# Sixteen DRAM copies of the B and C rows, and last states that enter a scan through its first token

## Chip, cores and metric

The kernel runs on one core of a Trainium2 chip. The metric is the device time of one execution in microseconds (us); the time before is the median of three runs, 13002.54 us (12999.16 to 13004.72). The engines are named as in the profile: PE is TensorE with its weight loads (PEld), DVE is VectorE, ACT is ScalarE, POOL is GpSimd, and SP is SyncE, which issues the DMA transfers. DMA transfers run on 16 DMA engines.

## What is computed

The input is two images of 96 channels and 128 x 128 pixels. A layer normalization over the channels is followed by a mixer, two feed-forward blocks in rounded arithmetic and a 3 x 3 convolution between them. Nearly all of the time goes to the mixer, which sends the 16384 pixels of an image, as a sequence, through four state-space scans: by rows, by rows backwards, by columns, by columns backwards. Cut to what matters, one scan is:

```
def _mamba(x, in_w, conv_w, conv_b, xproj_w, dt_w, dt_b, A_log, Dp, outp_w):
    xc, z = jnp.split(x @ in_w.T, 2, axis=-1)           # 192 channels each
    xc = silu(causal_conv4(xc) + conv_b)
    xdbl = xc @ xproj_w.T
    dt_raw, Bm, Cm = xdbl[..., :6], xdbl[..., 6:22], xdbl[..., 22:]
    dt = softplus(dt_raw @ dt_w.T + dt_b)
    A = -jnp.exp(A_log)                                 # 192 channels x 16 states
    def step(h, t):
        dt_t, u_t, B_t, C_t = t
        h = exp(dt_t[:, :, None] * A) * h + dt_t[:, :, None] * B_t[:, None, :] * u_t[:, :, None]
        return h, einsum('bds,bs->bd', h, C_t)
    _, ys = jax.lax.scan(step, h0, (dt, xc, Bm, Cm))
    y = (ys + Dp * xc) * silu(z)
    return y @ outp_w.T
```

For every token and every one of 16 states, B and C are one number each, the same for all 192 channels of a direction.

## The kernel before

For each of two images, `normalize` writes the normalized image to DRAM by rows and by columns, `mamba` does the four scans, and `ffn_and_conv` the rest. `mamba` takes the directions in two pairs (the two forward ones, then the two backward ones). A pair's 2 x 192 channels lie in three groups of 128 partitions: group 0 is of the first direction, group 2 of the second, and group 1 has 64 channels of each. The sequence is cut into 32 pieces of 512 tokens. A step is one piece of one pair, so there are 64 steps for an image and 128 in all.

A step has 24 units: for each group, eight pairs of states. For one unit:

- POOL multiplies dt * u by the two rows of B (`b_part`, line 324, 128 x 1024).
- ACT makes the two decays exp(dt * A) (`decay`, line 330) in PSUM.
- DVE runs two scans of 512 tokens (`scan`, line 334), in place in the decays' tile. The state at the end of the preceding piece is the scan's initial value, read per partition from the tile `hst`; in the first step of a pair it is the constant 0.0.
- DVE multiplies both results by the rows of C (line 409), ACT saves the last states in `hst` (line 410), and PE sums the products over the states into y by products with the identity (`sums`, line 341).

When a group ends, DVE multiplies y by the gate (`gated`, line 349), and after groups 1 and 2 PE projects the result (`project`) and ACT adds it to the image in `collect`.

The rows of B and C must stand in all 128 partitions. `rows_out` (line 255) copies 64 rows of 512 tokens, 32 for B and 32 for C, from PE's result into SBUF (partitions 32 to 95 of the tile `rows`) and writes them to DRAM (`bcd`), in four copies by four transfers (line 261). `row_tile` (line 312) then reads tiles of 128 partitions x 4 rows x 512 tokens (1 MiB, 8 KB a partition) with one transfer for groups 0 and 2, in which partition p reads copy p mod 4, and two transfers of 64 partitions for group 1. One tile serves two units; there are 12 for B and 12 for C in a step. A tile of B is asked for 6 units ahead, one of C 4 units ahead, each into a ring of tiles, so that a transfer waits until an old tile has been used.

All engines run in the order in which the program issues: the schedule is written out by hand in the loop over k, the units of all steps (lines 436 to 457). In turn k the loop issues, in this order: a fetch of B (for unit k + 6, at even k), POOL's multiply of unit k + 2 (`feed`), the work put down for (k, 0), the first scan of unit k, the multiply by C and the rest of unit k - 1 (`behind`), the second scan of unit k, a fetch of C (for unit k + 4), the decays of unit k + 2 (`feed_decay`), and the work put down for (k, 1). The work put down is the prologue of the next step (lines 301 to 310): convolution and gate on PE, in turns 4 to 7, 10 and 11; silu on ACT in turns 8 and 14; the rows in turn 12; and for each group the softplus that makes dt, begun in turns 13, 18 and 21, whose last four instructions (`dt_q`, `dt_log`, `dt_sum`, `dt_u`; lines 287 to 297, 128 x 512) run on POOL between its multiplies.

Of the kernel before, what the change touches and what calls it, by code (L numbers as in the profile page):

```python
# [10 lines left out]
F32 = mybir.dt.float32  # L11
# [3 lines left out]
AF = mybir.ActivationFunctionType  # L15
ALU = mybir.AluOpType
# [7 lines left out]
T = 512  # L24
NT = L // T
R = T // W
S = 16
# [2 lines left out]
HID = 384  # L30
PAIRS = ((0, 2), (1, 3))
NG = 3
COPIES = 4
B_AHEAD = 3
C_AHEAD = 2
AHEAD = 2
# [1 line left out]
BCO = 32  # L38
NBC = 4 * S
# [3 lines left out]
def tile_metaformer(ctx: ExitStack, tc: tile.TileContext, a: dict, out: bass.AP):  # L43
    nc = tc.nc
# [30 lines left out]
    amat = cpool.tile([128, 2, NG, S], F32, name="amat")  # L75
# [107 lines left out]
    def mamba(acc, xnr, xnc):  # L183

        with ExitStack() as st:
            pool = lambda n, bufs, **kw: st.enter_context(tc.tile_pool(name=n, bufs=bufs, **kw))
            io, one, two, gen = pool("io", 1), pool("one", 1), pool("two", 2), pool("gen", 4)
            ps_w, ps_y, ps_m = (pool(n, k, space=PSUM) for n, k in (("ps_w", 3), ("ps_y", 1), ("ps_m", 1)))
            rows_d = pool("rows_d", 3, space=DRAM)

            hst = one.tile([128, NG, S], F32, name="hst")
            acc_w = acc.rearrange("c (h w) -> c w h", w=W)

            def misc():
# [15 lines left out]
            def prologue(pi, i, d):  # L210
# [3 lines left out]
                src = []  # L214
# [40 lines left out]
                def rows_out():  # L255

                    d["rows"] = one.tile([BCO + NBC, T], F32, name="rows")
                    nc.scalar.copy(d["rows"], d["ps"][0 : BCO + NBC, :])
                    d["bcd"] = rows_d.tile([COPIES, 2, NBC // 2, T], F32, name="bcd")
                    for n in range(COPIES):  # L260
                        nc.sync.dma_start(d["bcd"][n].rearrange("k r t -> (k r) t"), d["rows"][BCO:, :])

# [35 lines left out]

                at = [(0, 0, load), (8, 1, partial(silu, "xc")), (14, 1, partial(silu, "sz"))]
                at += [(12, 0, rows), (12, 1, rows_out)]
                for g, k in enumerate((4, 5, 6)):
                    at += [(k, 0, partial(conv, g)), (k, 1, partial(conv_out, g))]
# [7 lines left out]
            def row_tile(d, g, s, k, ahead):  # L312

                t = gen.tile([128, 4, T], F32, name=f"row{k}", bufs=ahead + 1)
                for half in range(2) if g == 1 else (slice(None),):
                    rows = slice(half * 64, half * 64 + 64) if g == 1 else half
                    at = s + S * (half if g == 1 else g // 2)
                    n = (64 if g == 1 else 128) // COPIES
                    src = d["bcd"][None, :, k, at : at + 4, :].broadcast_to((n, COPIES, 4, T))
                    nc.sync.dma_start(t[rows], src)  # L320
                return t

            def b_part(d, g, b):
                nc.gpsimd.tensor_tensor(b, d["dtu"][g][:, None, :].broadcast_to((128, 2, T)), b, ALU.mult)  # L324

            def decay(pi, d, g, s):

                da = ps_w.tile([128, 2, T], F32, name="da")
                for j in range(2):
                    nc.scalar.activation(da[:, j, :], d["dt"][g], AF.Exp, scale=amat[:, pi, g, s + j : s + j + 1])  # L330
                return da

            def scan(i, g, s, j, da, b, h):
                nc.vector.tensor_tensor_scan(  # L334
                    h[:, j, :], da[:, j, :], b[:, j, :],
                    0.0 if i == 0 else hst[:, g, s + j : s + j + 1], ALU.mult, ALU.add,
                )

            def sums(s, y, c):
                for j in range(2):  # L340
# [27 lines left out]
            steps = [(pi, i) for pi in range(2) for i in range(NT)]  # L368
            units = [(g, s) for g in range(NG) for s in range(0, S, 2)]
            nu = len(units)  # L370
            total = nu * len(steps)
            state = [{} for _ in steps]
            todo = {}

            def later(k, where, f, *args):
                todo.setdefault((k, where), []).append(partial(f, *args))

            def issue(k, where):
                for f in todo.pop((k, where), ()):
                    f()  # L380
# [3 lines left out]
            bs, cs, das, hs = {}, {}, {}, {}  # L384

            def fetch(k, n, ahead, m):
                if k < total:
                    t = row_tile(state[k // nu], *units[k % nu], n, ahead)
                    m[k], m[k + 1] = t[:, 0:2, :], t[:, 2:4, :]

            def feed(k):
                if k < total:
                    n = k // nu
                    b_part(state[n], units[k % nu][0], bs[k])

            def feed_decay(k):
                if k < total:
                    n = k // nu
                    das[k] = decay(steps[n][0], state[n], *units[k % nu])
# [3 lines left out]
            def behind(k):  # L403

                n, u = divmod(k, nu)
                (pi, i), d, (g, s) = steps[n], state[n], units[u]
                h, c = hs.pop(k), cs.pop(k)
                if (g, s) not in BY_POOL:
                    nc.vector.tensor_tensor(c, h, c, ALU.mult)  # L409
                nc.scalar.copy(hst[:, g, s : s + 2], h[:, :, T - 1])  # L410
                if s == 0:
                    if k > 0:
                        pn, pu = divmod(k - 1, nu)
                        gated(steps[pn][0], state[pn], units[pu][0], ys.pop(k - 1))
                    y = ps_y.tile([128, T], F32, name="y")
                    nc.tensor.matmul(y, dmat[:, pi, g, :], d["xc"][:, g, :], start=True, stop=False)  # L416
                else:
                    y = ys.pop(k - 1)
                ys[k] = y
                if (g, s) in BY_POOL:  # L420
                    later(k + 1, 1, by_pool, s, y, h, c)
                else:
                    sums(s, y, c)
                if k == total - 1:
                    gated(pi, d, g, y)
                if s == S - 2 and g > 0:
                    later(k + 4, 0, project, pi, i, d, g)
                    later(k + 4, 1, collect, pi, d, g)
# [4 lines left out]
            for k in range(AHEAD):  # L433
                feed(k)
                feed_decay(k)
            for k in range(total + 6):
                n, u = divmod(k, nu)
                if u == 0 and n + 1 < len(steps):
                    for m, where, f in prologue(*steps[n + 1], state[n + 1]):
                        later(k + m, where, f)  # L440
                if k % 2 == 0:
                    fetch(k + 2 * B_AHEAD, 0, B_AHEAD, bs)
                feed(k + AHEAD)
                issue(k, 0)
                if k < total:
                    (_, i), (g, s) = steps[n], units[u]
                    da, b = das.pop(k), bs.pop(k)
                    hs[k] = b if (g, s) in BY_POOL else da
                    scan(i, g, s, 0, da, b, hs[k])
                if 0 < k <= total:  # L450
                    behind(k - 1)
                if k < total:
                    scan(i, g, s, 1, da, b, hs[k])
                if k % 2 == 0:
                    fetch(k + 2 * C_AHEAD, 1, C_AHEAD, cs)
                feed_decay(k + AHEAD)
                issue(k, 1)
# [99 lines left out]
    for b in range(NB):  # L557
        acc = accp.tile([C, L], F32, name="acc")
        xnr = dpool.tile([C, L], F32, name="xnr")
        xnc = dpool.tile([C, L], F32, name="xnc")  # L560
        normalize(b, acc, xnr, xnc)
        mamba(acc, xnr, xnc)
        ffn_and_conv(b, acc)
# [59 lines left out]
```

## Time and profile before

| what | value |
|---|---|
| span of the profiled run | 13002.5 us |
| DVE busy | 11569.1 us (89%) |
| PE busy | 10850.3 us (83%) |
| POOL busy | 9215.4 us (71%) |
| ACT busy | 8560.0 us (66%) |
| POOL's multiplies by B, line 324 | 3072 x 2358 ns |
| POOL idle before them, for DMA row<-bcd | 1419.2 us |
| DVE's multiplies by C, line 409 | 3072 x 1206 ns |
| transfers row<-bcd | 2048 of 1024 KB (7.5 us to landing), 2048 of 512 KB (8.0 us) |
| transfers bcd<-rows | 512 of 128 KB (9.8 us to landing) |
| DMA queue of these transfers | 3394.12 MB, 83.1% of 16 engines' span |
| HBM read, written | 3288.94 MB, 104.86 MB |

A line of the page's groups names the source line, the engine, the operation, what is written and read, the shape and the count; then the busy time and the mean of one; then how long the engine stood idle just ahead of it, and what ended most of that idle time. Idle time of an engine that sets no pace costs nothing. A timeline row gives the start and the length of one instruction, or of several alike in a row (x2, x3), and in brackets the engine's idle time ahead of it with what ended it. The landing of a transfer is counted from its issue on SP.

### The profile page before, as it was taken

Reading aid. Unit: us, or ns where it says so; the run is one execution under the profiler, and the core shown is the slowest. Engines: PE = TensorE matmul, PEld = TensorE weight load, DVE = VectorE, ACT = ScalarE, POOL = GpSimd, SP = SyncE. Lnnn points to the kernel's source line nnn. Section 1 sums busy time; section 2 is a strip of 40 time slices with the busy share of each in tenths; the row PEclk is TensorE's granted clock in tenths of the full one; section 3 lists DMA queues with packets and bytes.
Section 4 is the critical chain, followed back from the end, with each engine's and each line's share of the span. In section 5 each row is a group of like instructions: output and inputs, shape, how many; then the busy total and the mean of one; then the engine's idle time right before and its main releaser. Section 6 shows DMA issues by size and latency. Waiting matters only on the chain. (4 is left out here: it accounts for less than half of the span.)

```text
span 13002.5 us, 97992 instructions
## 1 busy us (share of the span) xinstructions
PE 10850.3 (83%) x24208; PEld 3987.1 (31%) x24208; DVE 11569.1 (89%) x10865; ACT 8560.0 (66%) x14738; POOL 9215.4 (71%) x4772
## 2 busy tenths in 40 slices
PE   6888888888888888888978888888888888888889
PEld 2323233333333333333323333332333333333233
DVE  5999999999999999995459999999999999999954
ACT  6666666666666666665566666666666666666655
POOL 4877778777787787772147778777787777877721
PEclk8999999999999999999989999999999999999999
DMA  7999999999999999992079999999999999999920
GB/s 226 287 294 282 298 288 285 295 283 298 288 285 295 283 295 289 285 295 68 13 226 285 298 283 292 290 285 298 285 291 291 284 298 286 290 294 281 296 61 13
DMA packets 545331, 3400.40 MB, mean 262 GB/s; under 512 B 81612, under 2 KB 82732, under 8 KB 146840
## 3 DMA queue, kind: packets, MB, share of 16 engines
q1 hardware_dynamic: 544760, 3394.12, 83.1%
q8 instruction: 195, 3.19, 0.1%
q14 instruction: 376, 3.08, 0.1%
HBM read 3288.94 MB, written 104.86 MB: 261 GB/s over the span
## 5 line engine op out<-in xcount | busy, mean ns | idle before, releaser
L324 POOL TENSOR_TENSOR row<-dtu,row 128x1024 f32<-128x1024 f32 x3072 | 7175.7, 2358 | 1739.3 <-DMA row<-bcd 1419.2
L334 DVE TENSOR_TENSOR_SCAN da<-da,hst,row 128x512 f32<-128x512 f32 x5952 | 7339.4, 1274 | 351.2 <-ACT da L330 194.6
L341 PE MATMUL y<-row,ident 128*128 128x512 f32 x12288 | 6120.1, 626 | 1113.3 <-DVE row L409 1098.9
L330 ACT ACTIVATE da<-dt,amat 128x512 f32<-128x512 f32 x6144 | 4249.4, 692 | 207.5 <-ACT hst L410 0.4
L341 PEld LDWEIGHTS y<-row,ident 128*128 128x128 f32 x12288 | 2288.9, 197 | 4779.4 <-DVE row L409 2292.3
L409 DVE TENSOR_TENSOR row<-da,row 128x1024 f32<-128x1024 f32 x3072 | 3705.9, 1206 | 19.6 <-DMA row<-bcd 18.8
L410 ACT COPY hst<-da 128x2 f32<-128x2 f32 x3072 | 484.0, 158 | 2235.5 <-DVE row L409 2233.3
L416 PE MATMUL y<-xc,dmat 128*128 128x512 f32 x768 | 526.1, 773 | 779.1 <-DVE sz L349 779.1
L287 POOL TENSOR_TENSOR q<-e,q 128x512 f32<-128x512 f32 x384 | 488.0, 1271 | 821.8 <-ACT hst L410 709.1
L233 ACT ACTIVATE xc<-misc,convb 128x512 f32<-128x512 f32 x384 | 264.2, 688 | 1117.5 <-PE misc L207 1117.5
L207 PE MATMUL misc<-xa,inx 96*128 96x512 f32 (+1 forms) x2048 | 932.4, 597 | 59.0 <-DMA xa<-xnr 57.2
L207 PE MATMUL misc<-xb,inx 96*64 96x512 f32 (+1 forms) x2048 | 928.1, 595 | 1.6 <-ACT xc L233 1.6
L531 POOL TENSOR_TENSOR acc<-acc,y 96x512 f32<-96x512 f32 x128 | 147.6, 1153 | 987.0 <-DVE y L530 987.0
L541 PE MATMUL pc<-pad,kw 96*96 96x512 f32 x1152 | 566.7, 593 | 0.0
L207 PEld LDWEIGHTS misc<-xa,inx 96*128 96x128 f32 (+1 forms) x2048 | 323.6, 163 | 625.5 <-issue 493.4
L293 POOL TENSOR_TENSOR dt<-dt,ln 128x512 f32<-128x512 f32 x384 | 486.9, 1268 | 30.1
L297 POOL TENSOR_TENSOR dtu<-dt,xc 128x512 f32<-128x512 f32 x384 | 488.5, 1272 | 0.5
L290 POOL TENSOR_TENSOR ln<-ln,q 128x512 f32<-128x512 f32 x384 | 488.1, 1271 | 0.5
L359 PE MATMUL misc<-sz,gmat 128*96 128x512 f32 x1024 | 483.6, 594 | 0.0
L416 PEld LDWEIGHTS y<-xc,dmat 128*128 128x128 f32 x768 | 129.0, 211 | 1102.1 <-DVE sz L349 1099.1
L268 PE MATMUL misc<-rows,dtw 12*128 12x512 f32 x768 | 439.7, 652 | 18.5 <-ACT dt L275 17.2
L132 DVE TENSOR_TENSOR xq<-xm,rs 96x512 fp8e5<-96x512 f32 x128 | 87.9, 687 | 387.8 <-ACT rs L128 387.8
(75 smaller groups left out, 8403.8 us busy)
## 6 DMA issues: line engine op xcount, KB each, us to landing
row<-bcd SPq DMA_DIRECT2D x2048, 1024.0 KB, 7.5
row<-bcd SPq DMA_DIRECT2D x2048, 512.0 KB, 8.0
bcd<-rows SPq DMA_DIRECT2D x512, 128.0 KB, 9.8
xa<-xnr SPq DMA_DIRECT2D x124, 193.1 KB, 5.8
xb<-xnc SPq DMA_DIRECT2D x124, 193.1 KB, 5.5
acc<-in_x_dram SPq DMA_DIRECT2D x16, 768.0 KB, 17.8
xnr<-xn SPq DMA_DIRECT2D x16, 768.0 KB, 4.3
xnc<-stg SPq DMA_DIRECT2D x16, 768.0 KB, 5.6
```

The costliest lines, as they stand in the source:

```text
L207: nc.tensor.matmul(ps[rows, :], w(PAIRS[pi][d], k, lo, hi), src[d][:, k : k + T], **se)
L287: nc.gpsimd.tensor_tensor(d["q"], d["e"], d["q"], ALU.subtract)
L290: nc.gpsimd.tensor_tensor(d["ln"], d["ln"], d["q"], ALU.add)
L293: nc.gpsimd.tensor_tensor(d["dt"][g], d["dt"][g], d["ln"], ALU.add)
L297: nc.gpsimd.tensor_tensor(dtu, d["dt"][g], d["xc"][:, g, :], ALU.mult)
L324: nc.gpsimd.tensor_tensor(b, d["dtu"][g][:, None, :].broadcast_to((128, 2, T)), b, ALU.mult)
L330: nc.scalar.activation(da[:, j, :], d["dt"][g], AF.Exp, scale=amat[:, pi, g, s + j : s + j + 1])
L334: nc.vector.tensor_tensor_scan(h[:, j, :], da[:, j, :], b[:, j, :], 0.0 if i == 0 else hst[:, g, s + j : s + j + 1], ALU.mult, ALU.add,)
L341: nc.tensor.matmul(y, ident, c[:, j, :], start=False, stop=s + j == S - 1)
L409: nc.vector.tensor_tensor(c, h, c, ALU.mult)
L416: nc.tensor.matmul(y, dmat[:, pi, g, :], d["xc"][:, g, :], start=True, stop=False)
L541: nc.tensor.matmul(pc, kw[:, t, :], rows, start=t == 0, stop=t == 8)
```

## The change

Two things are changed in `mamba`.

First, `bcd` holds 16 copies of each direction's rows in place of four copies of all rows. It is laid out as [B or C, 32 copies, 17 rows, 512 tokens]: the first 16 copies are of the first direction, the other 16 of the second, and a seventeenth row is left free between copies. Each of four transfers now takes 16 rows (B or C of one direction) and writes each of them 16 times. A tile is always read by one transfer of 128 partitions, each copy into eight neighbouring partitions; group 1 takes copies 8 to 23 and so gets both directions in one transfer.

Second, a scan always starts from 0.0. What the old state adds to the first token, exp(dt_0 * A) * h, is put into that token's input: `entering` makes it for a group (one exponential on ACT and one multiply on POOL, 128 x 16, once a step and group), and `b_part` adds it to the first token of both rows (one POOL instruction of 128 x 2 for each unit). The first steps of a pair have no such part. It is for shorter scan instructions on DVE, which read no operand per partition.

```
-COPIES = 4
+COPIES = 16
...
+            enter = one.tile([128, NG, S], F32, name="enter")
...
-                    d["bcd"] = rows_d.tile([COPIES, 2, NBC // 2, T], F32, name="bcd")
-                    for n in range(COPIES):
-                        nc.sync.dma_start(d["bcd"][n].rearrange("k r t -> (k r) t"), d["rows"][BCO:, :])
+                    d["bcd"] = rows_d.tile([2, 2 * COPIES, S + 1, T], F32, name="bcd")
+                    for n in range(4):
+                        to = d["bcd"][n // 2, n % 2 * COPIES : (n % 2 + 1) * COPIES, 0:S, :]
+                        r = d["rows"][BCO + n * S : BCO + (n + 1) * S, None, :].broadcast_to((S, COPIES, T))
+                        nc.sync.dma_start(to.rearrange("n s t -> s n t"), r)
...
-                for half in range(2) if g == 1 else (slice(None),):
-                    rows = slice(half * 64, half * 64 + 64) if g == 1 else half
-                    at = s + S * (half if g == 1 else g // 2)
-                    n = (64 if g == 1 else 128) // COPIES
-                    src = d["bcd"][None, :, k, at : at + 4, :].broadcast_to((n, COPIES, 4, T))
-                    nc.sync.dma_start(t[rows], src)
+
+                src = d["bcd"][k, COPIES // 2 * g : COPIES // 2 * g + COPIES, None, s : s + 4, :]
+                nc.sync.dma_start(t, src.broadcast_to((COPIES, 128 // COPIES, 4, T)))
                 return t
 
-            def b_part(d, g, b):
+            def entering(pi, d, g):
+
+                nc.scalar.activation(enter[:, g, :], amat[:, pi, g, :], AF.Exp, scale=d["dt"][g][:, 0:1])
+                nc.gpsimd.tensor_tensor(enter[:, g, :], enter[:, g, :], hst[:, g, :], ALU.mult)
+
+            def b_part(i, d, g, s, b):
                 nc.gpsimd.tensor_tensor(b, d["dtu"][g][:, None, :].broadcast_to((128, 2, T)), b, ALU.mult)
+                if i > 0:
+                    nc.gpsimd.tensor_tensor(b[:, :, 0], b[:, :, 0], enter[:, g, s : s + 2], ALU.add)
...
-            def scan(i, g, s, j, da, b, h):
-                nc.vector.tensor_tensor_scan(
-                    h[:, j, :], da[:, j, :], b[:, j, :],
-                    0.0 if i == 0 else hst[:, g, s + j : s + j + 1], ALU.mult, ALU.add,
-                )
+            def scan(j, da, b, h):
+                nc.vector.tensor_tensor_scan(h[:, j, :], da[:, j, :], b[:, j, :], 0.0, ALU.mult, ALU.add)
...
+                    if steps[n + 1][1] > 0:
+                        for g in range(NG):
+                            later(k + nu - 4 + nu // NG * g, 1, entering, steps[n + 1][0], state[n + 1], g)
```

The work of `entering` is put down in turns 20 of a step, and 4 and 12 of the next.

More of the change, by code (lines that the diff above doesn't have):

```diff
@@ L393, in feed @@
                     n = k // nu
-                    b_part(state[n], units[k % nu][0], bs[k])
+                    b_part(steps[n][1], state[n], *units[k % nu], bs[k])
             def feed_decay(k):
@@ L445, in mamba @@
                 if k < total:
-                    (_, i), (g, s) = steps[n], units[u]
+                    (g, s) = units[u]
                     da, b = das.pop(k), bs.pop(k)
                     hs[k] = b if (g, s) in BY_POOL else da
-                    scan(i, g, s, 0, da, b, hs[k])
+                    scan(0, da, b, hs[k])
                 if 0 < k <= total:
@@ L452, in mamba @@
                 if k < total:
-                    scan(i, g, s, 1, da, b, hs[k])
+                    scan(1, da, b, hs[k])
                 if k % 2 == 0:
```

## The prediction

> **What bounds the kernel now.** I read the page first (shares, groups), then the instructions of the scan's line, then the timelines of VectorE (DVE), GpSimd (POOL), TensorE (PE) and SyncE through one step, then the table by stretch. DVE is busy 89% of the span, and POOL 71%; the mean does not say that POOL has no slack in part of each step. From the page's groups:
>
> ```profile
> L334 DVE TENSOR_TENSOR_SCAN da<-da,hst,row 128x512 f32<-128x512 f32 x5952 | 7339.4, 1274 | 351.2 <-ACT da L330 194.6
> ```
>
> A step (512 tokens of one pair) is 24 units; a unit is two scans and one multiply on DVE. I number units 0 to 23; 24 to 28 are the next step's 0 to 4. On DVE's timeline of one step in the steady state:
>
> ```profile
> 10026.50 1.29 DVE L334 TENSOR_TENSOR_SCAN da<-da,hst,row 128x512 f32<-128x512 f32 x1 [1.75 <-ACT da L330]
> 10030.23 0.69 DVE L349 TENSOR_TENSOR sz<-y,sz 128x512 f32<-128x512 f32 x1 [1.32 <-PE y L341]
> ...
> 10041.30 2.45 DVE L334 TENSOR_TENSOR_SCAN da<-da,hst,row 128x512 f32<-128x512 f32 x2
> 10044.79 2.45 DVE L334 TENSOR_TENSOR_SCAN da<-da,hst,row 128x512 f32<-128x512 f32 x2
> ...
> 10066.56 1.21 DVE L409 TENSOR_TENSOR row<-da,row 128x1024 f32<-128x1024 f32 x1
> 10067.68 2.45 DVE L334 TENSOR_TENSOR_SCAN da<-da,hst,row 128x512 f32<-128x512 f32 x2
> ...
> 10096.17 2.45 DVE L334 TENSOR_TENSOR_SCAN da<-da,hst,row 128x512 f32<-128x512 f32 x2
> ```
>
> A unit takes 3.49 us (10041.30 to 10044.79). A step takes about 90.1 us: 24 x 3.49, 3 gatings of 0.6, and some 4.4 of stalls, at units 8 to 9 (behind PE and ACT, the first two lines) and 16 to 17 (ACT's table loads). POOL's timeline of the same step:
>
> ```profile
> 10056.27 1.27 POOL L287 TENSOR_TENSOR q<-e,q 128x512 f32<-128x512 f32 x1 [6.25 <-ACT hst L410]
> ...
> 10059.80 1.27 POOL L290 TENSOR_TENSOR ln<-ln,q 128x512 f32<-128x512 f32 x1
> 10061.15 1.26 POOL L293 TENSOR_TENSOR dt<-dt,ln 128x512 f32<-128x512 f32 x1
> ...
> 10065.90 7.00 POOL L324 TENSOR_TENSOR row<-dtu,row 128x1024 f32<-128x1024 f32 x3
> ...
> 10094.46 16.30 POOL L324 TENSOR_TENSOR row<-dtu,row 128x1024 f32<-128x1024 f32 x7
> ```
>
> From 10056.27 POOL never rests: twelve softplus instructions lie between the multiplies of units 18 to 28. The multiply of unit 20 (first of the x3) ends at 68.26 and its scan starts at 68.86 (second of the pair at 67.68); that of unit 28 ends at 96.82, its scan starts at 97.35. Slack: 0.6 and 0.5 us. PE has none between units 3 and 9, as the table by stretch shows. Its columns: the stretch, its length, busy time of PE, weight loads, DVE, ACT and POOL with their instructions, PE's clock, DMA share, GB/s:
>
> ```profile
> 10010.00:10015.00 5.00, 5.00 (x13) 2.01 (x11) 5.00 (x6) 2.31 (x5) 5.00 (x3) 1.00 0.76 164
> ...
> 10032.00:10044.00 12.00, 11.71 (x28) 4.01 (x27) 12.00 (x12) 8.63 (x16) 4.67 (x2) 1.00 1.01 246
> 10058.00:10067.00 9.00, 6.16 (x10) 2.33 (x11) 9.00 (x9) 4.75 (x9) 8.92 (x6) 0.81 1.01 421
> ```
>
> PE is busy for all 5.00 us of the first. With the DMA engines full, the 64-row halves of group 1 move at 246 GB/s (the stretch holds some full tiles), 128-row tiles at 421: a full tile takes 1.05 MB / 0.425 = 2.45 us. DMA rarely holds up DVE, since tiles are asked for about 14 us ahead.
>
> [...] For reads out of SBUF, the 96-row stores of xn hold packets of 309, about 600 and 900 ns for 8 KB[...]. [...] The trace shows tiles landing in order of issue.
>
> **The change part by part.** *Scans lose the pointer.* The first step of each pair already starts from 0.0:
>
> ```profile
> L334 DVE TENSOR_TENSOR_SCAN da<-da,hst,row x5952: 1257/1276/1293, 253.0 to 12421.9; 128x512 f32<-128x512 f32 x199
> L334 DVE TENSOR_TENSOR_SCAN da<-da,row x192: 1201/1217/1232, 168.2 to 9630.0; 128x512 f32<-128x512 f32 x192
> ```
>
> 59 ns less per scan; start to start a unit takes 3.36 there. 2976 units x 0.125 = 372 us if DVE set the pace everywhere. It does not: units 3 to 9 follow PE, 14 to 17 ACT, 18 to 28 POOL. What stays is about 4 units (10 to 13), 0.5 us a step.
>
> *One add per unit on POOL.* From starts, 1024 elements cost 2.33 us and 512 cost 1.22, so an empty instruction 0.12; 128x2 costs about that. It waits for the multiply just ahead on POOL: the pair at 59.80 and 61.15, which waits so, takes 1.35, 0.13 over 1.22. Together 0.26 (bounds: 0.12 with no wait, and 0.5, twice my value, since no POOL instruction in the trace has rows of one element). Queued behind it are the next multiply and the softplus instructions, and DVE's scan waits for it. Three more multiplies of 128x16 cost 0.16 each a step, and their wait for ACT is over by then. Over units 18 to 28: 11 x 0.26 + 0.16 = 3.0 us against a slack of 0.5.
>
> *ACT's three exponentials a step* (128x16, about 0.2 us each) fall in units 20, 4 and 12, where ACT has idle time before PE's or DVE's results: nothing. *Group 1 as one transfer* spares 16 half tiles a step at about half rate, but DVE hardly waited for them: nothing, except that the queue is now empty at unit 12.
>
> *The copies.* Four writes a step stay, of 512 KB in place of 128 KB. SyncE's queue:
>
> ```profile
> 10045.29 2.47 SPq L261 DMA_DIRECT2D bcd<-rows  x4
> 10047.87 27.03 SPq L320 DMA_DIRECT2D row<-bcd  x8
> ```
>
> Before, each write read 64 partitions, and the four went at full rate (1.3 us in all). Now each reads 16 partitions,[...] 16 times over[...]. A 2 KB packet that takes 84 ns alone then takes about 4 x 77 (8 KB in 309 ns is 2 KB in 77). 64 packets an engine x 0.31 = 19.8 us in which nothing behind moves. Bounds: 5.4 us (64 x 84 ns[...]) and 21.5 (4 x 84). The C tile of unit 16 is issued at 44.7, just ahead, on an empty queue, and lands at about 49.2 (the quickest landing of a tile in the trace is 4.3 us); then the writes to 69.0, then one tile per 2.45: B of unit 20 at 71.5, C of 18 at 73.9, B22 76.4, C20 78.8, B24 81.3.
>
> DVE needs C18 at 66.56 (the multiply above): 7.3 late. From there 3.36 a unit: scan 25 (86.3 before) starts 6.6 late, unit 25's multiply 6.5. POOL starts unit 20 at 71.5, not 65.9; with the adds unit 25 ends at 92.1 (scan 25 is then at 93.0: hidden), unit 28 at 104.9, 7.6 late. PE's full stretch starts from unit 25's multiply and ends in the gating at unit 9, so 6.5 remains there; DVE's own 7.6 sinks in the 3 us of stalls before that gating. Less 0.5 for units 10 to 13: 6.0 us a step. The B tile of unit 24 must now wait on SyncE for all four writes (69.0, issued at 62 before); behind it wait C tiles, but the transfers are queued till then anyway. Sum: 126 steps x 6.0 = 756, and the first step of each of the two passes has nothing ahead of it to hide 18.5 us more of writes: 37. 13,003 + 793 = about 13,800.
>
> **The rivals.** *Writes hidden* (up to 13 us[...]): POOL alone. Unit 25 is late by 8 x 0.26 + 0.16 - 1.44 = 0.8, PE carries that to unit 9, minus 0.5: 0.3 us a step, 13,040; with adds of 0.5 it is 2.2 us a step, 13,270. [...] Against: the xn stores. *DVE sets the pace, faster*: writes hidden and the add nearly free. Units 18 to 25 give 1.0 and units 10 to 13 0.5: 1.5 us x 124 = 190, 12,815. Against: the slack of 0.5. *Tiles at half rate*:[...] 24 x 4.9 + 20 + 2 = 140 us a step, over 19,000. For: the split is not visible in the trace; against: the old 32 x 4 source kept full rate.
>
> **How the numbers follow.** Forecast 0.68; hidden with POOL 0.13; faster 0.11; half rate 0.08. The forecast's own spread (21.5 us of writes, dearer adds, partial hiding) is 13,400 to 14,400. The range takes in the hidden case, from 13,000, to 14,400, and leaves out the faster case and the half rate. Faster by over 0.2%: 0.12; within: 0.04; slower: 0.84.
>
> **What would show it.** Scans of 1217 ns; writes that take some 20 us from first to last landing; DMA share near 1 at 100 GB/s in units 13 to 19; DVE's multiply waiting for DMA row<-bcd by about 7 us once a step; POOL's adds near 0.25 us. Wrong would be: writes landing within 13 us, DVE's multiply waiting for nothing, or tiles that take 5 us.

## The result, and the profile after

| kernel | median us | lowest to highest | ratio to before (95% interval) |
|---|---|---|---|
| before | 13002.48 | 12999.16 to 13004.72 | 1 |
| changed | 15242.42 | 15151.14 to 15275.81 | 1.1712 (1.1661 to 1.1762) |

The changed kernel is 17% slower. The direction was forecast, the size was not: 15,242 us lies above the range of 13,000 to 14,400. Over the 126 steps of the prediction's sum the extra 2,240 us are 17.8 us a step, where the forecast had 6.0.

The page's groups of the changed kernel show where it goes. The first is of the kernel before, DVE's multiply by C. Those below it are of the changed kernel: POOL's multiply, the scan, DVE's multiply by C and the new add.

```profile
L409 DVE TENSOR_TENSOR row<-da,row 128x1024 f32<-128x1024 f32 x3072 | 3705.9, 1206 | 19.6 <-DMA row<-bcd 18.8 <-DVE da L334 0.4
```

```profile
L329 POOL TENSOR_TENSOR row<-dtu,row 128x1024 f32<-128x1024 f32 x3072 | 7221.8, 2351 | 3489.1 <-DMA row<-bcd 3061.4
L341 DVE TENSOR_TENSOR_SCAN da<-da,row 128x512 f32<-128x512 f32 x6144 | 7183.4, 1213 | 225.3 <-POOL row L329 168.8
L413 DVE TENSOR_TENSOR row<-da,row 128x1024 f32<-128x1024 f32 x3072 | 3731.8, 1215 | 2980.5 <-DMA row<-bcd 2952.6
L331 POOL TENSOR_TENSOR row<-row,enter 128x2 f32<-128x2 f32 x2976 | 577.3, 194 | 233.3
```

The scan does become shorter (1213 ns a scan; it was 1274 with the pointer). But DVE's multiply by C now waits 2952.6 us for DMA, where it was 18.8 before. POOL's wait for DMA doubles, from 1419.2 to 3061.4. DVE's idle time ahead of all scans fell from 532 us (351.2 ahead of those with the pointer, 180.9 ahead of the 192 that start from 0.0 before, too) to 225, and that ahead of these multiplies rose from 20 to 2,980: DMA sets the pace. The page's row of the DMA queue and its table of transfers say the same. The columns of the first are packets, MB, and share of 16 engines' time; of the others, count, size and time from issue to landing.

```profile
q1 hardware_dynamic: 626680, 3595.38, 92.5%
```

```profile
row<-bcd SPq DMA_DIRECT2D x3072, 1024.0 KB, 19.0
bcd<-rows SPq DMA_DIRECT2D x512, 512.0 KB, 17.6
```

The bytes rose by 6% (3394 to 3595 MB), but the DMA engines' time rose from 83.1% of 13,002 us to 92.5% of 15,274, which is 31% more. So each byte takes longer. The table by stretch, with half a step that lies between two steps' writes, has the rate (same columns as in the prediction; the last two are DMA share and GB/s):

```profile
12072.00:12078.00 6.00, 4.03 (x10) 1.35 (x8) 6.00 (x7) 1.83 (x5) 5.81 (x5) 1.00 1.04 311
12078.00:12127.00 49.00, 32.42 (x56) 11.34 (x55) 34.01 (x31) 23.68 (x45) 36.61 (x31) 0.86 1.02 229
```

In the second stretch the DMA engines are full for 49 us and move 229 GB/s. A tile of 1.05 MB takes 1.05 / 0.229 = 4.6 us there; the prediction took 2.45 from 421 GB/s. The first stretch holds the end of the four writes and moves more, not less. In the packet records an 8 KB packet of a tile has a median of 544 ns, and 314 before. DVE's timeline shows what it does to one step:

```profile
12077.85 2.33 DVE L341 TENSOR_TENSOR_SCAN da<-da,row 128x512 f32<-128x512 f32 x2
12086.42 1.23 DVE L413 TENSOR_TENSOR row<-da,row 128x1024 f32<-128x1024 f32 x1 [6.24 <-DMA row<-bcd]
...
12095.58 1.23 DVE L413 TENSOR_TENSOR row<-da,row 128x1024 f32<-128x1024 f32 x1 [2.31 <-DMA row<-bcd]
```

The first wait is that of unit 18, where about 7 us were forecast; it is 6.9 us a step on average. But DVE waits at most of the other C tiles too: 1285 times for 1536 C tiles, 23.0 us a step in all. The kernel uses a tile (of B or C) each 3.4 us, and one arrives each 4.6. 24 tiles by 4.6 us are 110 us, a little more than the 90.1 + 17.8 = 107.9 us of a step.

### The profile page after: what moved, and what is told of

Its sections match the earlier page's. It is cut to its first block, busy times and chain, and to the rows that moved or that the text cites. A ratio compares the mean times of both kernels' runs of the same rounds, so it can differ in the third digit from the quotient of the medians.

```text
span 15274.0 us, 99408 instructions
## 1 busy us (share of the span) xinstructions
PE 11705.2 (77%) x24208; PEld 4211.3 (28%) x24208; DVE 11320.2 (74%) x10865; ACT 8701.8 (57%) x15110; POOL 9859.5 (65%) x8120
## 3 DMA queue, kind: packets, MB, share of 16 engines
q1 hardware_dynamic: 626680, 3595.38, 92.5%
## 5 line engine op out<-in xcount | busy, mean ns | idle before, releaser
L329 POOL TENSOR_TENSOR row<-dtu,row 128x1024 f32<-128x1024 f32 x3072 | 7221.8, 2351 | 3489.1 <-DMA row<-bcd 3061.4
L345 PE MATMUL y<-row,ident 128*128 128x512 f32 x12288 | 6868.0, 693 | 2171.5 <-DVE row L413 2167.9
L341 DVE TENSOR_TENSOR_SCAN da<-da,row 128x512 f32<-128x512 f32 x6144 | 7183.4, 1213 | 225.3 <-POOL row L329 168.8
L413 DVE TENSOR_TENSOR row<-da,row 128x1024 f32<-128x1024 f32 x3072 | 3731.8, 1215 | 2980.5 <-DMA row<-bcd 2952.6
L345 PEld LDWEIGHTS y<-row,ident 128*128 128x128 f32 x12288 | 2497.6, 216 | 6385.6 <-DVE row L413 3744.5
L420 PE MATMUL y<-xc,dmat 128*128 128x512 f32 x768 | 560.4, 819 | 1002.0 <-DVE sz L353 1002.0
L208 PE MATMUL misc<-xa,inx 96*128 96x512 f32 (+1 forms) x2048 | 978.0, 622 | 186.8 <-DMA xa<-xnr 120.6
L331 POOL TENSOR_TENSOR row<-row,enter 128x2 f32<-128x2 f32 x2976 | 577.3, 194 | 233.3
## 6 DMA issues: line engine op xcount, KB each, us to landing
xa<-xnr SPq DMA_DIRECT2D x124, 193.1 KB, 19.8
```

What stands on the lines that cost most here:

```text
L208: nc.tensor.matmul(ps[rows, :], w(PAIRS[pi][d], k, lo, hi), src[d][:, k : k + T], **se)
L331: nc.gpsimd.tensor_tensor(b[:, :, 0], b[:, :, 0], enter[:, g, s : s + 2], ALU.add)
L341: nc.vector.tensor_tensor_scan(h[:, j, :], da[:, j, :], b[:, j, :], 0.0, ALU.mult, ALU.add)
L345: nc.tensor.matmul(y, ident, c[:, j, :], start=False, stop=s + j == S - 1)
```

## The experiments

Two theories of the slow tiles were put against each other. **A, the SBUF side:** a source of 16 copies by 8 repeats is slower to write into the tile's partitions than 32 repeats by 4 copies. **B, HBM:** the reads out of DRAM became slow, because 16 copies 34 KB apart are read in place of four. Beside them stood the questions of the prediction: what the writes cost, what the adds cost, and what the shorter scan gives.

### Transfers by themselves

A small kernel holds nothing but groups of transfers; POOL fills the tile with a memset between groups, so that its idle time ahead of a memset is the duration of the group. It computes nothing of the reference. Its core, for groups of eight tiles of 1 MiB (`n` counts them):

```
             # the old order: 32 repeats x 4 copies
+            nc.sync.dma_start(big[:, n], cp4[None, :, 0, 4 * (n % 4) : 4 * (n % 4) + 4, :].broadcast_to((32, 4, 4, T)))
...
             # the new order: 16 copies x 8 repeats
+            nc.sync.dma_start(big[:, n], cp16[0, 0:16, None, 4 * (n % 4) : 4 * (n % 4) + 4, :].broadcast_to((16, 8, 4, T)))
...
             # the same copies in the old order
+            nc.sync.dma_start(big[:, n], cp16[0, None, 0:4, 4 * (n % 4) : 4 * (n % 4) + 4, :].broadcast_to((32, 4, 4, T)))
...
             # 32 copies x 4 repeats
+            nc.sync.dma_start(big[:, n], cp32[0, 0:32, None, 4 * (n % 4) : 4 * (n % 4) + 4, :].broadcast_to((32, 4, 4, T)))
...
             # the new order into DRAM in place of SBUF
+            nc.sync.dma_start(plain[n].rearrange("(c b) a t -> c b a t", b=8), cp16[0, 0:16, None, 4 * (n % 4) : 4 * (n % 4) + 4, :].broadcast_to((16, 8, 4, T)))
...
             # the writes of 512 KB out of 16 partitions each, four of them
+            to = cp16[n // 2, n % 2 * 16 : (n % 2 + 1) * 16, 0:S, :]
+            nc.sync.dma_start(to.rearrange("n s t -> s n t"), big[32 + 16 * n : 48 + 16 * n, 0, 0:1, :].broadcast_to((S, 16, T)))
```

> The kernel computes nothing of the reference: it only runs groups of 1 MiB transfers, one kind of access per group, each group alone in the DMA queue. Theory A[...] Then a tile takes about 2.5 us from the old source (32 repeats x 4 copies), from 4 of the 16 copies read as 32 x 4, from 32 copies x 4 repeats and from 128 distinct rows; about 4.5 us from 16 copies x 8 repeats, whether the copies are 34 KB apart or packed at 8 KB; and between two DRAM tensors the 16 x 8 and the 32 x 4 source cost the same. Theory B (HBM)[...] Then 32 copies x 4 is slow too, the packed 16 x 8 differs from the spaced one, and between DRAM tensors 16 x 8 is slower than 32 x 4. On writes out of SBUF: [...]512 KB from 16 partitions takes 4.9 us; otherwise 1.3 us. [...]stores of 96 rows with 64 KB and 66 KB between rows are alike; if from the spacing, the 66 KB ones run at full rate.

POOL's timeline of this kernel; the number in brackets is the duration of the group ahead, with the latency of the last landing. In order: old order, new order, new copies in the old order, 32 copies by 4, sixteen halves of 64 partitions, four writes of 512 KB, four writes of 128 KB out of 64 partitions:

```profile
174.15 13.75 POOL L73 MEMSET big<- 128x16384 f32 x1 [22.47 <-DMA big<-cp]
227.77 13.75 POOL L73 MEMSET big<- 128x16384 f32 x1 [39.87 <-DMA big<-cp]
264.03 13.75 POOL L73 MEMSET big<- 128x16384 f32 x1 [22.51 <-DMA big<-cp]
300.57 13.75 POOL L73 MEMSET big<- 128x16384 f32 x1 [22.79 <-DMA big<-cp]
...
444.48 13.75 POOL L73 MEMSET big<- 128x16384 f32 x1 [39.20 <-DMA big<-cp]
...
566.09 13.75 POOL L73 MEMSET big<- 128x16384 f32 x1 [16.82 <-DMA cp<-big]
...
614.50 13.75 POOL L73 MEMSET big<- 128x16384 f32 x1 [4.06 <-DMA cp<-big]
```

Eight tiles take 22.47 us in the old order and 39.87 in the new one. The same sixteen copies read in the old order take 22.51, so neither their number nor their spacing matters: packed 8 KB apart they take 40.47 in the new order. The new order costs as much as sixteen halves of 64 partitions (39.20). The packets agree: one of 8 KB takes 577 ns on average in the new order and 572 in the halves, and 317 in the old order. What is left to HBM is settled by SyncE's timeline, where each group of eight DRAM to DRAM transfers begins at its issue and the next single issue comes when it has landed. L101 is the new order, L106 the old one.

```profile
469.92 5.34 SPq L101 DMA_DIRECT2D plain<-cp  x8
497.96 0.34 SPq L103 DMA_DIRECT2D big<-plain  x1
498.34 5.13 SPq L106 DMA_DIRECT2D plain<-cp  x8
530.57 0.33 SPq L108 DMA_DIRECT2D big<-plain  x1
```

With DRAM as the destination the new order takes 28.0 us and the old one 32.2: the loss is gone. It belongs to the SBUF side, and the HBM theory falls.

The four writes take 16.82 us (16.86 with sixteen different rows in place of one repeated), against 4.06 for the old ones. They do not move at one rate, as the table by stretch shows (busy time of DVE and POOL, PE's clock, DMA share, GB/s):

```profile
550.50:554.50 4.00, 0.00 (x0) 0.00 (x0) 1.00 0.93 102
554.50:557.50 3.00, 0.00 (x0) 0.00 (x0) 1.00 0.94 133
557.50:560.50 3.00, 0.00 (x0) 0.00 (x0) 1.00 0.95 207
```

The first write moves at 102 GB/s, and its 2 KB packets take 295 ns, close to the 308 of the prediction, whose factor of 4 (4 x 77 ns) no trace had shown until then. After it the rate rises, and packets of 155 and of 84 ns stand beside those of 295. The four writes come out of four different sets of partitions, and they overlap. So one write is as slow as was predicted, but four in a row take less than four times as long. In the other direction, one MiB read into 16 partitions took 11.78 us. With some 2 us of latency off (the small writes land 2.2 us after their issue) that is an estimated 107 GB/s, about the rate of the first write.

### The two halves of the change

One kernel has the 16 copies and the one-transfer tiles, with before's scans. The other has the constant start, `entering` and the adds, with before's copies and tiles.

```
 # the copies alone, against before
-COPIES = 4
+COPIES = 16
...
+                    d["bcd"] = rows_d.tile([2, 2 * COPIES, S + 1, T], F32, name="bcd")
...
+                src = d["bcd"][k, COPIES // 2 * g : COPIES // 2 * g + COPIES, None, s : s + 4, :]
+                nc.sync.dma_start(t, src.broadcast_to((COPIES, 128 // COPIES, 4, T)))
```

```
 # the scans alone, against before
+            def entering(pi, d, g):
...
+                if i > 0:
+                    nc.gpsimd.tensor_tensor(b[:, :, 0], b[:, :, 0], enter[:, g, s : s + 2], ALU.add)
...
-                    0.0 if i == 0 else hst[:, g, s + j : s + j + 1], ALU.mult, ALU.add,
+                nc.vector.tensor_tensor_scan(h[:, j, :], da[:, j, :], b[:, j, :], 0.0, ALU.mult, ALU.add)
```

> The kernel before with the sixteen copies and their one-transfer tiles alone, scans and POOL as before. If the tile transfers set the pace, about 15,200 us (15,050 to 15,350), like the changed kernel. If POOL's adds carry part of the loss, clearly less: below 15,000.

> The kernel before with the scan change alone (constant start, POOL's adds), copies as before. By the prediction's POOL chain (units 18 to 28 without slack) 0.3 us a step are lost: 13,040 us (12,990 to 13,270). If DVE set the pace, it would be faster: 12,630 if in every unit, 12,815 if the adds were nearly free.

The copies alone give 15309.42 us, 1.1768 (1.1747 to 1.179); the scans alone 13070.28 us, 1.0049 (1.0036 to 1.0063). The copies carry the whole loss: their interval overlaps that of the full change. The 0.5% of the scans is not on top of it, since in a step that DMA paces the adds lie in waiting time: DVE waits for them 20.8 us in the changed kernel, and 397 with the scans alone.

POOL's timeline with the scans alone has the price of the add, measured from start to start:

```profile
10030.83 2.35 POOL L331 TENSOR_TENSOR row<-dtu,row 128x1024 f32<-128x1024 f32 x1
10033.27 0.19 POOL L333 TENSOR_TENSOR row<-row,enter 128x2 f32<-128x2 f32 x1
10033.41 2.36 POOL L331 TENSOR_TENSOR row<-dtu,row 128x1024 f32<-128x1024 f32 x1
```

Multiply and add together take 10033.41 - 10030.83 = 2.58 us, and a multiply alone 2.33: the add costs 0.25, the prediction's 0.26. DVE's table of waits names who pays for it:

```profile
DVE da L343 <- POOL row L333: 397.0, 614, 1.6
```

397 us in 614 waits, 3.1 us a step, nearly all of it in units 20, 24, 25, 27 and 28, where the prediction had seen no slack. That is more than the 372 us which the shorter scans could give if nothing else held DVE.

### The old order of reading, with the new writes

The changed kernel, but its tiles are read as 32 repeats of 4 of the copies, with group 1 in halves as before. All sixteen copies are still written.

```
-src = d["bcd"][k, COPIES // 2 * g : COPIES // 2 * g + COPIES, None, s : s + 4, :]
-nc.sync.dma_start(t, src.broadcast_to((COPIES, 128 // COPIES, 4, T)))
+for half in range(2) if g == 1 else (slice(None),):
...
+    src = d["bcd"][k, None, c0 : c0 + 4, s : s + 4, :].broadcast_to((n, 4, 4, T))
+    nc.sync.dma_start(t[rows], src)
```

> The changed kernel with sixteen copies written as it does, but tiles read in the old way: partition p reads copy p mod 4 of four of the sixteen, group 1 in two halves. Theory A and theory B: tiles take 2.5 us again, and the time is that of scan_only plus what 4 writes of 512 KB cost: under 13,200 us if they move at full rate (5 us in all), about 13,800 if they take 20 us as predicted. If the layout with 34 KB between copies is slow by itself, over 14,000.

13935.49 us, 1.0712 (1.0698 to 1.0727). The order of reading alone is worth 15,242 - 13,935 = 1,307 us. What remains is 865 us over the scans alone, 6.9 us a step, and it is the stall that the prediction had worked out, on DVE's timeline:

```profile
12083.95 2.51 DVE L345 TENSOR_TENSOR_SCAN da<-da,row 128x512 f32<-128x512 f32 x2
12094.87 1.22 DVE L417 TENSOR_TENSOR row<-da,row 128x1024 f32<-128x1024 f32 x1 [8.41 <-DMA row<-bcd]
```

One wait of 8.4 us, once a step, in the multiply of unit 18 (the prediction had 7.3 us for it). The four writes landed at 12077.6, 12082.2, 12085.9 and 12088.3, the B tile behind them at 12092.3 and the C tile of unit 18 at 12094.8. The writes' 2 KB packets take 163 ns on average over the run, 84 when alone.

### The same, with each write's rows laid four partitions apart in SBUF

The rows of the four writes stand interleaved, so that 16 rows of one write lie four partitions apart, from 32 to 95, in place of side by side. The columns of the weight that makes the rows are put into the same order. Bytes and packets are the same.

```
-r = d["rows"][BCO + n * S : BCO + (n + 1) * S, None, :].broadcast_to((S, COPIES, T))
+r = d["rows"][BCO:, :].rearrange("(s n) t -> n s t", n=4)[n][:, None, :].broadcast_to((S, COPIES, T))
```

> old_order with one change: the 64 rows lie interleaved in SBUF, so that the 16 rows of one write stand on every fourth of partitions 32 to 95[...]. [...]the writes take about 5.4 us and hide: 13,070 us (13,030 to 13,200). If the number of bytes written costs it, it stays near 13,900.

13073.02 us, 1.0054 (1.0041 to 1.0068), as with the scans alone (1.0049). 862 of the 865 us are gone. DVE's multiplies by C wait 78.0 us for DMA, where they waited 1143.0 with the rows side by side; what leads its waits in the scans is the add on POOL:

```profile
DVE da L345 <- POOL row L335: 373.1, 569, 1.6
```

Four times the bytes written cost nothing measurable by themselves. The cost was their coming out of 16 neighbouring partitions (13,935 us against 13,073).

### Both repairs of the transfers, with before's scans

On the kernel with the copies alone: 32 copies of a direction in place of 16, so that a copy goes into four neighbouring partitions; one transfer per tile; interleaved rows. It should show whether one transfer for group 1 is worth anything once nothing is slow.

```
-COPIES = 16
+COPIES = 32
...
+r = d["rows"][BCO:, :].rearrange("(s n) t -> n s t", n=4)[n][:, None, :].broadcast_to((S, COPIES, T))
```

> The kernel before (its own scans) with 32 copies of each direction, each read into four partitions, every tile in one transfer, and interleaved rows: twice the bytes written of the changed kernel, a source of 32 x 4 in place of 16 x 8. [...] tiles at 2.5 us and writes of 11 us that hide: 13,000 us (12,950 to 13,100). If reading a copy of one's own is what is slow, tiles stay at 4.5 us and the time is above 15,000.

13110.13 us, 1.0083 (1.0067 to 1.0098), just above what was expected. Its tiles land in 7.4 us, where those of the copies alone took 18.8, so the rate is back. But it writes 1 MiB four times a step in place of 128 KB, and DVE's stalls are 5.0 us a step against 4.3. Of this 0.59 is a wait for DMA at unit 18, behind the writes. One transfer for group 1 shows no gain, and there was little to win: in the kernel before DVE's multiplies waited for tiles 18.8 us in all. What it is worth with before's small writes, no run shows.

### What the shorter scan would give if the add were free

The scans alone, with the adds and `entering` left out, so that every piece starts from a zero state. It leaves out the carry of states from piece to piece.

```
-                if i > 0:
-                    nc.gpsimd.tensor_tensor(b[:, :, 0], b[:, :, 0], enter[:, g, s : s + 2], ALU.add)
...
-                    if steps[n + 1][1] > 0:
-                        for g in range(NG):
-                            later(k + nu - 4 + nu // NG * g, 1, entering, steps[n + 1][0], state[n + 1], g)
```

> scan_only without the adds and without what feeds them, so a piece starts from zero: the state carried over between pieces is left out. It is the whole gain that shorter scans can give here. By the prediction 1.0 us a step in units 18 to 25 and 0.5 in units 10 to 13: 12,815 us. If DVE set the pace in every unit: 12,630. If POOL's slack of 0.5 us caps units 18 to 28 as a whole: about 12,880.

12812.99 us, 0.9854 (0.9841 to 0.9868). The scans' whole gain is 1.5 us a step, half of the 3.0 that 24 x 0.125 us would make. The group of its scans names what takes the place:

```profile
L341 DVE TENSOR_TENSOR_SCAN da<-da,row 128x512 f32<-128x512 f32 x6144 | 7233.0, 1214 | 611.0 <-POOL row L331 256.5 <-ACT da L337 213.7 <-ACT hst L414 128.1
```

DVE is idle 611 us ahead of scans, and 532 in the kernel before. In the 124 steps that take over a state its stalls grow by 1.1 us a step: 0.7 ahead of scans, for POOL's multiply, and 0.4 in the multiplies by C, for DMA. Its waits for ACT and PE stay as they were. The other 0.4 us of the missing gain were not traced.

### The carry in the middle group alone

By the prediction units 18 to 28 have no room on POOL. Group 1, units 8 to 15, lies wholly outside of them, and no softplus stands between its multiplies. This kernel is before, with the constant start, `entering` and the adds for group 1 only; the diff is against the kernel with the scans alone.

```
-                if i > 0:
+                if i > 0 and g == 1:
                     nc.gpsimd.tensor_tensor(b[:, :, 0], b[:, :, 0], enter[:, g, s : s + 2], ALU.add)
...
-                nc.vector.tensor_tensor_scan(h[:, j, :], da[:, j, :], b[:, j, :], 0.0, ALU.mult, ALU.add)
+                    0.0 if i == 0 or g == 1 else hst[:, g, s + j : s + j + 1], ALU.mult, ALU.add,
...
-                        for g in range(NG):
-                            later(k + nu - 4 + nu // NG * g, 1, entering, steps[n + 1][0], state[n + 1], g)
+                        later(k + nu - 4 + nu // NG, 1, entering, steps[n + 1][0], state[n + 1], 1)
```

> The kernel before with constant start and adds for group 1 alone (units 8 to 15), where POOL has 5 us of slack or more; groups 0 and 2 keep their scans. By the prediction's steps only units 10 to 13 gain: 12,940 us (12,900 to 12,980). If the adds cost wherever they stand, no faster than before.

12922.47 us, 0.9937 (0.9925 to 0.995): faster than before by 80 us, and the only version here that carries all states and beats both kernels. This is the group of its scans with a constant start:

```profile
L343 DVE TENSOR_TENSOR_SCAN da<-da,row 128x512 f32<-128x512 f32 x2176 | 2566.5, 1214 | 401.6 <-ACT da L339 211.5 <-POOL row L331 167.9 <-issue 18.1
```

The 167.9 us behind POOL lie in the first steps of the passes, nearly all of them. In the steps that take over a state DVE waits for no add.

### One edit at a time from the changed kernel

First the interleaved rows alone, then 32 copies as well.

```
+r = d["rows"][BCO:, :].rearrange("(s n) t -> n s t", n=4)[n][:, None, :].broadcast_to((S, COPIES, T))
...
-COPIES = 16
+COPIES = 32
```

> The changed kernel with interleaved rows alone; tiles still read as 16 x 8. If its loss is the tiles' half rate (24 x 4.5 us and more a step), no change: 15,240 us (15,100 to 15,330). If the writes' 16 partitions carry a part of it, as they did for old_order (865 us), clearly less, down to 14,400.

> after_spread with 32 copies in place of 16, so that each copy goes into four partitions (a source of 32 x 4) and twice the bytes are written. [...] tiles at full rate again, and the losses of spread32 (108 us) and scan_only (64 us) together: 13,170 us (13,080 to 13,250). If one tile per transfer or copies of one's own were slow, above 14,500.

With the rows interleaved: 15091.88 us, 1.16 (1.158 to 1.162), 150 us less than the changed kernel. No change had been expected; it is 1.2 us a step, so the writes do take a small part. With 32 copies as well: 13101.5 us, 1.0074 (1.0057 to 1.0091). The one constant is worth 1,990 us, although it doubles the bytes written. Its line in the table of transfers:

```profile
row<-bcd SPq DMA_DIRECT2D x3072, 1024.0 KB, 7.6
```

Tiles land 7.6 us after their issue, where the changed kernel had 19.0.

## Why the prediction was wrong

**The step that failed: "then one tile per 2.45".** The prediction took the rate of a tile, 421 GB/s, from 32 x 4 sources and carried it over to the 16 x 8 source. (1.05 MB at 421 GB/s are 2.5 us rather than 2.45, which changes nothing here.) Its third rival had tiles of 4.9 us, twice the 2.45, which no trace had shown, at a chance of 0.08, and the argument set against it ("the old 32 x 4 source kept full rate") was evidence on another shape. Tiles that take 5 us were among the prediction's own signs of being wrong, and they take 4.6. The transfers by themselves show the step wrong (22.47 to 39.87 us for eight tiles), and one constant in the changed kernel shows that this is what costs the time there (15,092 to 13,102 us). The prediction worked out what 16 partitions do to the writes and left the rate of the tiles as it was, though these are twelve times the bytes (24 MiB against 2 a step).

What makes the new order slow is not shown: no trace tells which DMA engine moves which partitions of a tile, and that its 39.87 us come close to the 39.20 of the halves of 64 partitions is a likeness of two times, no more. Shown is that the order of the dimensions of a transfer into SBUF sets its rate: the same sixteen copies took 39.87 us in the new order and 22.51 in the old one.

**The sizes of the third rival** were also off: it had 4.9 us a tile, 20 for the writes and 2 more, 140 us a step. A tile took 4.6, which is 110 for 24 of them, and a step took 107.9: the writes added next to nothing. In the changed kernel their 2 KB packets lie spread over some 10 us (12066 to 12077) among packets of tiles. They take 91 ns on average there and 96 over the run, little over the 84 when alone. And while they pass, the tiles are faster: in the middle of that time an 8 KB packet takes 309 ns in place of 544, and from 12067 to 12076 the queue moves 367 GB/s. Interleaving the rows gave only 1.2 us a step. Why the writes are fast there no run shows, so it stays open.

**Slow writes out of 16 partitions: right, mis-sized, and not binding.** With the order of reading put back, the kernel is the one that the forecast described: 13,935 us measured, 13,800 forecast, one stall per step of 8.4 us, 7.3 forecast. With the rows four partitions apart the stall is gone. The forecast's net of 6.0 us a step measured 6.9. That the sizes came out so near is partly luck, for two errors cancel. The term was 19.8 us for four writes; they took 14.1 from the first packet to the last, since they overlap (102 GB/s at first and up to 207 when alone). And they start later than was worked out. The prediction let the C tile of unit 16 land at 49.2, on an empty queue, but in the same step of the kernel before it landed at 54.96, 10.3 us after its issue: other tiles stood ahead of it, the last of which landed at 52.49. Writes that begin some 6 us later and take 5.7 us less end where they were forecast to.

**One add per unit on POOL: right.** 0.25 us measured, 0.26 worked out. The rival "writes hidden, POOL alone" had 13,040; the scans alone gave 13,070, so this half of the change costs 0.2 us a step more than the 0.3 that were worked out.

**The scan's gain and its cap: right in size.** 1213 ns a scan (1217 expected), and 12,813 us without the adds, where the rival "DVE sets the pace, faster" had 12,815. The prediction's account of which engine holds which units also led to the version that gains, with adds in group 1 alone: 12,940 us expected, 12,922 measured.

**"Group 1 as one transfer: nothing": right as far as the runs show.** With tiles at full rate and one transfer each, nothing is gained (13,110 us), but more bytes are written there, so this part doesn't stand alone.

**Where the time went, in sum.** Of the 2,240 us, 1,990 go with the shape of the tiles' source, 150 with the place of the writes' rows in SBUF, and 99 (13,101 - 13,002) are left, with the adds and the larger writes still in. Alone, the scans with their adds cost 68 us (13,070) and the 32 copies 108 (13,110), so these parts do not add up. The order in which they are taken off matters: with full-rate tiles the same place of these rows costs 862 us (13,935 to 13,073), not 150.

## What to carry to other kernels

When a DMA source or destination gets a new order of its dimensions, treat its rate as unknown, even if bytes, packets and partitions stay as they were. Time eight such transfers alone before anything is built on them; here the order was worth 17 us in 40. And when a short instruction moves from a busy engine to another, look at its slack unit by unit: POOL, busy 71%, had no room for them in the units behind its softplus work, and moving them in group 1 alone, a third of the step, was what gained.

## What was not expected of the hardware

- A tile of 128 partitions moves at little over half the rate when its source is 16 copies by 8 repeats (39.87 us for eight) and at full rate as 32 copies by 4 (22.79) or 32 repeats by 4 copies (22.51). Into DRAM the slow order loses nothing (28.0 against 32.2 us).
- A write of 512 KB out of 16 partitions starts at 102 GB/s, with 2 KB packets of 295 ns, but four of them out of different partitions overlap: up to 207 GB/s, and 16.82 us in all.
- The 96-row stores, which hold packets of about 600 and 900 ns for 8 KB beside those of 309, are hardly faster with another spacing of rows in DRAM: eight with rows 64 KB apart took 22.70 us, and 22.55 with 66 KB. What the slow packets come from, no run shows.
- In the kernel with the old order the writes' packets took 163 ns, in the changed kernel 91 to 96, with the same writes, and there the tiles' packets became faster meanwhile (309 in place of 544 ns). Why stays open, as said above.
